# Last block's self-attention: the second maximum of a step issued behind VectorE's copies of the older step

## The chip, the cores and the metric

The kernel runs on one core of a Trainium2 chip. The metric is the device time of one execution in microseconds (us), the median of several runs. A core has five engines that run side by side, each through its own instructions in their order: TensorE (PE in the profile, matmuls and transposes; PEld are its weight loads), VectorE (DVE), ScalarE (ACT), GpSimd (POOL) and SyncE (SP, which here starts most transfers). Matmuls write to PSUM, a small memory from which VectorE and ScalarE read. An instruction that needs another engine's result waits for it, and everything behind it on its own engine waits too.

## What is computed

Four blocks follow each other on an input of 4 x 512 tokens of width 256, with a context of 4 x 64 tokens. The first three are a cross-attention block, a transformer block (self-attention with heads of 64, cross-attention, gated feed-forward), and four layers of a state-space model. The change lies in the last one, whose self-attention has 16 heads of 16:

```python
def _mha(q_in, kv_in, wq, bq, wk, bk, wv, bv, wo, bo):
    b = q_in.shape[0]
    q = (q_in @ wq.T + bq).reshape(b, -1, HEADS, HD).transpose(0, 2, 1, 3)
    k = (kv_in @ wk.T + bk).reshape(b, -1, HEADS, HD).transpose(0, 2, 1, 3)
    v = (kv_in @ wv.T + bv).reshape(b, -1, HEADS, HD).transpose(0, 2, 1, 3)
    scores = jnp.einsum('bhqd,bhkd->bhqk', q, k) * HD ** (-0.5)
    p = jax.nn.softmax(scores, axis=-1)
    o = jnp.einsum('bhqk,bhkd->bhqd', p, v)
    o = o.transpose(0, 2, 1, 3).reshape(b, -1, WIDTH)
    return o @ wo.T + bo
...
h = _layernorm(x, ln1_g, ln1_b)
x = x + _mha(h, h, sa_wq, sa_bq, sa_wk, sa_bk, sa_wv, sa_bv, sa_wo, sa_bo)
h = _layernorm(x, ln2_g, ln2_b)
x = x + _mha(h, context, ca_wq, ca_bq, ca_wk, ca_bk, ca_wv, ca_bv, ca_wo, ca_bo)
```

All of it is float32.

## The kernel before

Self-attention of both transformer-like blocks is written by `self_stage`, called once with `wide` true (heads of 64, in the second block) and once with `wide` false (heads of 16, in the last block, `layer3`). The order of all instructions is written by hand: the body stands under `tc.manual_schedule()`, and each engine gets its instructions in the order in which the Python code issues them.

The work of the last block is 16 chunks `c` of 128 query and key features, which with `wide` false hold 4 heads each (a head is padded to 32 of the 128 rows, `stride`). A chunk takes `spc` = 4 steps, one for each tile of 128 queries, so there are K = 64 steps. One step `k` does four heads of one query tile:

- `scores(k)` issues four matmuls of 32 rows, two into each of two PSUM tiles `ps_s` (name tag `big`, two buffers, so the tile of half `h` in step k+1 uses the buffer of half `h` in step k). Line L952.
- `softmaxed(k)` does, for each half `h`, the negated row maximum on VectorE (`nm`, L963, both heads of the half at once) and then two exps on ScalarE with the row sums as a second output (`pr`, `rs`, L967; the sums come out in an extra accumulator read). The exps are the last readers of the half's `ps_s`.
- `transposes(k, h)` transposes the half's two tiles of probabilities on TensorE into PSUM (`ps_pt`, tag `pt`, two buffers, L981), four transposes a tile, and copies each to `pT`: half 0 by ScalarE (L984), half 1 by VectorE (L986).
- `through_values(n)` multiplies transposed probabilities by values (`ps_o`, L1000). After eight of them a chunk is complete: `finish` copies it out on ScalarE (`AT`, L1018), spreads the row sums by matmul (`ps_rs`, L1025) and VectorE multiplies (L1035).

The steps are overlapped by one: in step `k` the loop issues transposes of step k-1 around the scores of step `k`. In between it works off pieces from queues held by `Pieces`: projections of query, key and value for a later group (L185, evicted by VectorE at L1818, L1820, L1827), output projections (`ps_wo`, evicted at L921), transposes of normalised features (`ps_tr`, tag `pt` too, evicted as `hT` at L646) and pieces of the layer normalisation (L612 to L622). `work()` issues the matmuls of at most one piece, `evict()` issues the VectorE instructions that empty the pieces issued before and moves the normalisation on by one. The pieces share one PSUM buffer (tag `mi`), except `ps_tr`.

So with `wide` false TensorE's order within step `k` is: transposes(k-1, 0), scores(k), one `through_values`, a first piece, transposes(k-1, 1), one `through_values`, a second piece. VectorE's order is: eviction of the second piece of step k-1, both maxima of step k, in every fourth step a reciprocal of the row sums, eviction of the first piece, the two copies of step k-1. ScalarE's is: two copies of step k-1, four exps of step k, in every fourth step the copy of `AT`.

In the loop below, `K` is 64 and `back` is true from the second step on.

Of the kernel before, what the change touches and what calls it, by code (L numbers as in the profile page):

```python
# [8 lines left out]
F32 = mybir.dt.float32  # L9
AF = mybir.ActivationFunctionType  # L10
ALU = mybir.AluOpType
AX = mybir.AxisListType
# [3 lines left out]
P = 128  # L16
B = 4
T = 512
# [39 lines left out]
class Pieces:  # L58
# [11 lines left out]
    def evict(self, norms=1):  # L70
        for ev, ps in self.pend:
            ev(ps)
        self.pend.clear()
        for _ in range(norms):
            if self.norms and next(self.norms[0], 0) == 0:
                self.norms.pop(0)
# [29 lines left out]
    def until(self, ok):  # L106
        for _ in range(200):
            if ok():
                return
            self.evict()  # L110
            if not ok():
                self.work()
        raise RuntimeError("a piece never comes")
# [11 lines left out]
def kernel(ctx: ExitStack, tc: tile.TileContext, t: dict, out: bass.AP):  # L125
    nc = tc.nc
# [478 lines left out]
    def norm(pool, src, b, xns, bias=None, key=None, tag="xn", lag=1):  # L605


        mv = pool.tile([P, TPB, 2], F32, name="ln_mv", tag="ln_mv", bufs=3)
        rstd = pool.tile([P, TPB], F32, name="ln_rstd", tag="ln_rstd", bufs=3)
        for j in range(TPB):  # L610
            st = pool.tile([P, 6], F32, name="ln_st", tag="ln_st", bufs=4)
            nc.vector.bn_stats(out=st, in_=src[:, b * TPB + j, :])  # L612
            nc.vector.bn_aggr(out=mv[:, j, :], in_=st)
            yield
        nc.vector.tensor_scalar(rstd, mv[:, :, 1], EPS, None, ALU.add)  # L615
        nc.gpsimd.tensor_tensor(rstd, rstd, mhalf, ALU.pow)  # L616
        for _ in range(lag):
            yield
        xn = src if tag is None else pool.tile([P, TPB, D], F32, name=tag, tag=tag)
        for j in range(TPB):  # L620
            i = b * TPB + j
            nc.vector.tensor_scalar(  # L622
                xn[:, j, :], src[:, i, :], mv[:, j, 0:1], rstd[:, j : j + 1], ALU.subtract, ALU.mult
            )
            if bias is not None:
                add_bias(src, bias, i)
            if j == TPB - 1:
                xns[b if key is None else key] = xn
            yield
# [223 lines left out]
    def self_stage(X, pool, psum, wide, project, values, Wo, ln, bias, at_end=None, side=None, follows=None, tail=None, fill=None):  # L853
# [72 lines left out]
        def begin(n):  # L926
            b, g = divmod(n, G)
            if g == 0:
                prep.extend(features(pool, psum, xns, hTs, b, c, ln) for c in range(DC))
            prep.extend(projected(n, 0, k) for k in range(2))  # L930
            prep.extend(value(n, j) for j in range(TPB))
            prep.extend(projected(n, m, k) for m in range(1, 4) for k in range(2))

        def combos(k):

            c, r = divmod(k, spc)
            if wide:
                return [(2 * r + i, j) for i in range(2) for j in range(2)]
            return [(r, j) for j in range(4)]

        prs, nms, sums = {}, {}, {}

        def scores(k):
            c = k // spc
            at["chunk"] = c
            until(lambda: c in qs and c in ks)
            for h in range(2):
                ps = psum.tile([P, 2, T], F32, name="ps_s", tag="big", bufs=2)
                for x in range(2):
                    i, j = combos(k)[2 * h + x]  # L950
                    q = slice(j * stride, (j + 1) * stride)
                    nc.tensor.matmul(ps[:, x, :], qs[c][q, i * P : (i + 1) * P], ks[c][q, :], start=True, stop=True)  # L952
                nms[k, h] = ps

        def softmaxed(k):
            c, r = divmod(k, spc)
            if r == 0:
                sums[c] = pool.tile([P, TPB * hpc], F32, name="rs", tag="rs", bufs=6 if wide else 3)
            rs = sums[c][:, 4 * r : 4 * r + 4]
            for h in range(2):  # L960
                ps = nms.pop((k, h))
                nm = pool.tile([P, 2], F32, name="nm", tag="nm", bufs=4)
                nc.vector.tensor_reduce(nm, ps, AX.X, ALU.max, negate=True)  # L963
                for x in range(2):
                    y = 2 * h + x
                    pr = prs[k, y] = pool.tile([P, T], F32, name="pr", tag="pr", bufs=6)
                    nc.scalar.activation(  # L967
                        pr, ps[:, x, :], AF.Exp, bias=nm[:, x : x + 1], accum_out=rs[:, y : y + 1]
                    )

        def transposes(k, h):
            c, r = divmod(k, spc)
            hc = 2 * c + combos(k)[0][0] // 2
            for x in range(2 * h, 2 * h + 2):
                i, j = combos(k)[x]
                if (hc, j) not in pTs:
                    pTs[hc, j] = pool.tile([P, TPB, W2], F32, name="pT", tag="pT", bufs=2 * hpc)
                pr = prs.pop((k, x))
                pp = psum.tile([P, TPB, P], F32, name="ps_pt", tag="pt", bufs=2)
                for t4 in range(TPB):  # L980
                    nc.tensor.transpose(pp[:, t4, :], pr[:, t4 * P : (t4 + 1) * P], ident)  # L981
                to = pTs[hc, j][:, :, (i % 2) * P : (i % 2 + 1) * P]
                if h == 0:
                    nc.scalar.copy(to, pp)  # L984
                else:
                    nc.vector.tensor_copy(to, pp)  # L986
# [56 lines left out]
        with tc.manual_schedule():  # L1043
            for _ in norm(pool, X, 0, xns, bias):
                pass
            begin(0)
            K = NG * SPG
            lead = 4 if wide else 2
            for k in range(K + 4):
                n, r = divmod(k, SPG)  # L1050
                if fill and k == K - SPG:
                    todo.fill.extend(fill(psum))
                if k < K and r == 0:
                    if n < NG - 1:
                        begin(n + 1)
                    else:
                        if follows:
                            norms.append(follows)
                    if n == NG - 1 and at_end:
                        prep.append((lambda: None, lambda ps: at_end(), None))  # L1060
                    if n % G == 0 and n // G < B - 1:
                        norms.append(norm(pool, X, n // G + 1, xns, bias, lag=6 if side else 1))
                evict()
                back = k and k <= K
                if back:
                    transposes(k - 1, 0)
                todo.work_aside()
                if k < K:
                    scores(k)
                    softmaxed(k)  # L1070
                if back and k % spc == 0:
                    rs = sums[k // spc - 1]
                    nc.vector.reciprocal(rs, rs)
                if wide:
                    work()
                    evict(0)
                todo.go_on(1)
                through_values(lead // 2)
                evict(0)
                if k % 2 or not todo.busy:  # L1080
                    todo.go_on(1)
                todo.work_aside()
                work()
                evict()
                if back:
                    transposes(k - 1, 1)
                todo.go_on(1)
                todo.work_aside()
                through_values(lead // 2)
                evict(0)  # L1090
                work()
                if back and (wide or (k - 1) % 2 == 1):
                    c, r1 = divmod(k - 1, spc)
                    hc = 2 * c + combos(k - 1)[0][0] // 2
                    pv.extend((hc, t4) for t4 in range(TPB))
            if tail:

                more = tail(psum)
                todo.evict(0)
                while at["wo"] < NG or more:  # L1100
                    work()
                    if more and (more[0][2] is None or more[0][2]()):
                        mm, ev, _ = more.pop(0)
                        todo.pend.append((ev, mm()))
                    evict(0)
            until(lambda: at["wo"] == NG)
            while todo.side or todo.aside or todo.pend:
                todo.work_aside()
                evict()
                todo.go_on(1)  # L1110
            assert todo.empty() and not pv
# [943 lines left out]
```

## Time and profile before

| what | us |
|---|---|
| median of 3 runs (4137.86 to 4146.58) | 4141.29 |
| the profiled execution | 4144.32 |
| its span, first to last instruction | 4142.5 |
| the changed stage, 64 steps, in the span | 3467 to 3885 |
| of it: TensorE busy | 384.4 |
| VectorE busy | 290.4 |
| ScalarE busy | 253.4 |
| maxima L963 in the stage: 128 of 1.22 | 150.8 |
| exps L967 in the stage: 256 of 0.69, and their accumulator reads, 256 of 0.20 | 172.6 and 51.9 |
| VectorE's copies L986: 127 of 0.68 | 81.4 |

Busy time is the union of an engine's instructions. Matmuls are pipelined and their ends are modelled, so a TensorE that is busy need not be at its peak; starts are more telling. In a timeline, a row is the start in us, the busy time, engine, line, operation, the tile written and those read, and their shapes; behind it, in brackets, stands how long the engine was idle before, and what ended that. Rows of one line that follow each other are merged (x8 is eight instructions). In a list of waits, a row is: the one that waited, what released it, and then the total in us, the number of waits and the longest.

Four score matmuls appear as eight records, since each float32 matmul is recorded as two.

### The profile page before, as it was taken

The numbers are of one execution on the slowest core, as the hardware profiler recorded it, in microseconds if no ns is written. First come the engines' busy times: TensorE is split into PE (matmuls) and PEld (weight loads), VectorE is DVE, ScalarE is ACT, GpSimd is POOL, SyncE is SP. The second block draws the span as 40 slices with busy tenths as digits, with TensorE's granted clock in tenths as the row PEclk, the third lists the DMA queues.
The fourth block names the chain that finished last, engine by engine and source line by source line (L and its number), as shares of the span: only waits on it lengthen the run. The fifth ranks groups of instructions, "written<-read, shape, count | busy, mean of one in ns | idle before, by whom it ended". The sixth has DMA issues, their size and how long they took to land. (4 is left out here: it accounts for less than half of the span.)

```text
span 4142.5 us, 48645 instructions
## 1 busy us (share of the span) xinstructions
PE 3515.9 (85%) x17616; PEld 2204.8 (53%) x17616; DVE 3033.5 (73%) x2903; ACT 2148.3 (52%) x4366; POOL 2388.4 (58%) x1625
## 2 busy tenths in 40 slices
PE   7989998988898897888888788888887667999889
PEld 4654554545566464555555555555554444555446
DVE  5547567476555633999999999998999996676653
ACT  2345454454212424666666666666666553556422
POOL 2349269076100425899999999999998881000131
PEclk8999999999998998988988898888888778999999
DMA  2023022033100203444444444444443441000000
GB/s 75 11 85 103 25 82 92 17 96 94 44 1 0 66 22 104 152 150 154 153 159 148 150 157 159 158 153 149 158 154 138 143 155 36 1 1 1 1 6 16
DMA packets 140287, 369.93 MB, mean 89 GB/s; under 512 B 20624, under 2 KB 38224, under 8 KB 140048
## 3 DMA queue, kind: packets, MB, share of 16 engines
q1 hardware_dynamic: 136688, 363.58, 26.1%
q10 hardware_dynamic: 3360, 3.25, 0.3%
q8 instruction: 139, 2.28, 0.2%
q14 instruction: 100, 0.82, 0.1%
HBM read 363.50 MB, written 3.28 MB: 89 GB/s over the span
## 5 line engine op out<-in xcount | busy, mean ns | idle before, releaser
L1632 POOL TENSOR_TENSOR dBu<-dtx,bB 128x1022 f32<-128x1022 f32 x512 | 1199.0, 2362 | 65.9 <-DVE ps_dA L1659 65.9
L1659 DVE TENSOR_TENSOR_SCAN ps_dA<-ps_dA,dBu 128x1024 f32<-128x1024 f32 x384 | 878.3, 2287 | 131.6 <-POOL dBu L1632 91.8
L1644 ACT ACTIVATE ps_dA<-dt,A 128x512 f32<-128x512 f32 x1024 | 708.3, 692 | 428.5 <-DVE hC L1666 365.6
L1692 PE MATMUL ps_y<-ident,hC 128*128 128x128 f32 x3072 | 460.7, 302 | 104.1 <-DVE hC L1666 104.0
L1692 PEld LDWEIGHTS ps_y<-ident,hC 128*128 128x128 f32 x3072 | 403.9, 158 | 193.3 <-DVE hC L1666 122.4
L1666 DVE TENSOR_TENSOR hC<-ps_dA,bC 128x1024 f32<-128x1024 f32 x384 | 470.1, 1224 | 25.5 <-issue 0.4
L967 ACT ACTIVATE pr<-ps_s,nm 128x512 f32<-128x512 f32 x512 | 345.2, 686 | 260.2 <-DVE nm L963 260.2
L963 DVE TENSOR_REDUCE nm<-ps_s 128x2 f32<-128x1024 f32 x256 | 301.4, 1218 | 158.5 <-PE ps_s L952 144.2
L1670 POOL TENSOR_TENSOR hP<-hP,bC 128x1024 f32<-128x1024 f32 x128 | 302.1, 2360 | 89.2 <-issue 38.9
L981 PE MATMUL ps_pt<-ident,pr 128*128 128x128 f32 x2048 | 284.9, 279 | 66.9 <-DVE pT L986 33.2
L981 PEld LDWEIGHTS ps_pt<-ident,pr 128*128 128x128 f32 x2048 | 232.2, 142 | 165.0 <-issue 61.7
L1659 DVE TENSOR_TENSOR_SCAN hP<-ps_dA,dBu 128x1024 f32<-128x1024 f32 x128 | 291.8, 2280 | 2.9 <-ACT dBu L1649 2.2
L616 POOL TENSOR_TENSOR ln_rstd<-ln_rstd,const 128x4 f32<-128x4 f32 x24 | 24.4, 1018 | 443.8 <-DVE ln_rstd L615 442.2
L178 PE MATMUL ps_cv<-xp,w_dg 128*128 128x512 f32 x512 | 248.9, 619 | 30.9 <-ACT dBu L1649 25.3
L535 DVE TENSOR_TENSOR_SCAN phb<-pdA,phb 128x512 f32<-128x512 f32 x128 | 223.8, 1763 | 60.3 <-POOL phb L525 43.8
L984 ACT COPY pT<-ps_pt 128x512 f32<-128x512 f32 x256 | 140.6, 592 | 171.5 <-PE ps_pt L981 170.9
L1000 PE MATMUL ps_o<-pT,V 128*64 128x256 f32 (+1 forms) x2048 | 221.8, 393 | 1.8 <-ACT AT L1018 1.8
L952 PE MATMUL ps_s<-kT,qT 64*128 64x512 f32 (+1 forms) x1024 | 208.3, 644 | 2.2 <-DVE kT L1172 1.4
L525 POOL TENSOR_TENSOR phb<-hT_res,pm 128x512 f32<-128x512 f32 x128 | 188.4, 1476 | 34.0 <-DMA pm<-scrp 20.9
L1692 PE MATMUL ps_y<-ident,hP 128*128 128x128 f32 x1024 | 154.1, 300 | 54.6 <-POOL hP L1670 54.6
L784 POOL TENSOR_TENSOR pr<-pr,rs 128x512 f32<-128x512 f32 x64 | 65.4, 1043 | 225.2 <-DVE rs L782 219.3
L1692 PEld LDWEIGHTS ps_y<-ident,hP 128*128 128x128 f32 x1024 | 132.2, 155 | 109.6 <-POOL hP L1670 63.1
(276 smaller groups left out, 6399.2 us busy)
## 6 DMA issues: line engine op xcount, KB each, us to landing
bB<-scr SPq DMA_DIRECT2D x256, 512.0 KB, 4.1
bC<-scr SPq DMA_DIRECT2D x256, 512.0 KB, 3.8
pm<-scrp SPq DMA_DIRECT2D x224, 256.0 KB, 3.1
w_pw_in<-in_L_in SPq DMA_DIRECT2D x7, 512.0 KB, 4.5
X<-in_x SPq DMA_DIRECT2D x4, 512.0 KB, 7.2
w_L_W<-in_L_W SPq DMA_DIRECT2D x2, 1024.0 KB, 10.4
w_L_Wq<-in_L_Wq SPq DMA_DIRECT2D x2, 1024.0 KB, 6.4
w_L_Wo<-in_L_Wo SPq DMA_DIRECT2D x2, 1024.0 KB, 9.0
```

Source lines behind the costliest of these rows:

```text
L178: nc.tensor.matmul(dst, l, r, start=(i == 0), stop=(i == len(pairs) - 1))
L535: nc.vector.tensor_tensor_scan(hb, dA, hb, 0.0, ALU.mult, ALU.add)
L963: nc.vector.tensor_reduce(nm, ps, AX.X, ALU.max, negate=True)
L967: nc.scalar.activation(pr, ps[:, x, :], AF.Exp, bias=nm[:, x : x + 1], accum_out=rs[:, y : y + 1])
L981: nc.tensor.transpose(pp[:, t4, :], pr[:, t4 * P : (t4 + 1) * P], ident)
L1000: nc.tensor.matmul(ps_o[0][j * stride : (j + 1) * stride, half * W2 : (half + 1) * W2], Vs[n][0][:, t4, h * stride : (h + 1) * stride], pT ...
L1632: nc.gpsimd.tensor_mul(dBu[:, :, 1:], dtx[:, 1:].unsqueeze(1).broadcast_to([P, 2, T - 1]), bmap[i // 2, 0][:, :, 1:])
L1644: nc.scalar.activation(dA, dt, AF.Exp, scale=A[:, l, m, s : s + 1])
L1659: nc.vector.tensor_tensor_scan(to, dA, dBus.pop(i).rearrange("p s t -> p (s t)"), 0.0, ALU.mult, ALU.add)
L1666: nc.vector.tensor_mul(hCs[i], dA, bmap[i // 2, 1])
L1670: nc.gpsimd.tensor_mul(hCs[i], hCs[i], bmap[i // 2, 1])
L1692: nc.tensor.matmul(y[:, j, k * P : (k + 1) * P], hC[:, s, j * P : (j + 1) * P], ident, is_transpose=True, start=False, stop=(2 * s2 + s == ...
```

## The change

`softmaxed` now takes the half `h` as a parameter and does one half. The first half is issued where both were. With `wide` true the second follows at once, as before. With `wide` false it is issued later in the step, behind `transposes(k - 1, 1)`: on VectorE the second maximum comes behind the reciprocal, the eviction of the step's first piece and the two copies of step k-1. Its two exps are issued there too; since no other ScalarE instruction lies in between, ScalarE's order doesn't change.

```diff
-        def softmaxed(k):
+        def softmaxed(k, h):
             c, r = divmod(k, spc)
-            if r == 0:
+            if r == 0 and h == 0:
                 sums[c] = pool.tile([P, TPB * hpc], F32, name="rs", tag="rs", bufs=6 if wide else 3)
             rs = sums[c][:, 4 * r : 4 * r + 4]
-            for h in range(2):
-                ps = nms.pop((k, h))
-                nm = pool.tile([P, 2], F32, name="nm", tag="nm", bufs=4)
-                nc.vector.tensor_reduce(nm, ps, AX.X, ALU.max, negate=True)
-                for x in range(2):
-                    y = 2 * h + x
-                    pr = prs[k, y] = pool.tile([P, T], F32, name="pr", tag="pr", bufs=6)
-                    nc.scalar.activation(
-                        pr, ps[:, x, :], AF.Exp, bias=nm[:, x : x + 1], accum_out=rs[:, y : y + 1]
-                    )
+            ps = nms.pop((k, h))
+            nm = pool.tile([P, 2], F32, name="nm", tag="nm", bufs=4)
+            nc.vector.tensor_reduce(nm, ps, AX.X, ALU.max, negate=True)
+            for x in range(2):
+                y = 2 * h + x
+                pr = prs[k, y] = pool.tile([P, T], F32, name="pr", tag="pr", bufs=6)
+                nc.scalar.activation(
+                    pr, ps[:, x, :], AF.Exp, bias=nm[:, x : x + 1], accum_out=rs[:, y : y + 1]
+                )
...
                 if k < K:
                     scores(k)
-                    softmaxed(k)
+                    softmaxed(k, 0)
+                    if wide:
+                        softmaxed(k, 1)
...
                 if back:
                     transposes(k - 1, 1)
+                if k < K and not wide:
+                    softmaxed(k, 1)
                 todo.go_on(1)
```

## The prediction

> **What bounds the kernel now.** I read the page first, then the table of stages, the waits inside the last block's self-attention, and last the timeline of single steps. The change touches only that stage: 64 steps from 3467 to 3885 us of a span of 4142.5.
>
> ```profile
> 3467.00:3885.00 418.00, 384.37 (x3316) 219.97 (x3316) 290.39 (x398) 253.37 (x655) 22.79 (x27) 1.00 0.00 1
> PE ps_pt L981 <- DVE pT L986: 21.3, 24, 1.6
> PE ps_pt L981 <- DVE hT L646: 6.4, 6, 1.6
> PE ps_s L952 <- DVE kT L1820: 0.8, 1, 0.8
> ```
>
> First line: TensorE (PE) is busy 384 of 418 us, VectorE (DVE) 290, ScalarE (ACT) 253, granted clock 1.00, no DMA. The others are PE's waits in the stage (total, times, longest). Most are transposes that wait for VectorE's copies; the scores never wait for an exp. The first wait is what the change goes for. The absence of the other is what I doubt will last.
>
> A step with no extra piece of work (a "bare" step), start and duration in us:
>
> ```profile
> 3558.67 1.14 PE L952 MATMUL ps_s<-kT,qT 32*128 32x512 f32 x8
> 3559.74 0.64 PE L1000 MATMUL ps_o<-pT,V 128*32 128x256 f32 x8
> 3559.84 2.36 DVE L963 TENSOR_REDUCE nm<-ps_s 128x2 f32<-128x1024 f32 x2 [1.19 <-PE ps_s L952]
> 3560.31 1.09 PE L981 MATMUL ps_pt<-ident,pr 128*128 128x128 f32 x8
> 3561.16 0.69 ACT L967 ACTIVATE pr<-ps_s,nm 128x512 f32<-128x512 f32 x1 [1.75 <-DVE nm L963]
> 3561.84 0.68 ACT L967 ACTIVATE pr<-ps_s,nm 128x512 f32<-128x512 f32 x1
> 3562.11 1.28 DVE L986 COPY pT<-ps_pt 128x512 f32<-128x512 f32 x2
> 3562.50 0.69 ACT L967 ACTIVATE pr<-ps_s,nm 128x512 f32<-128x512 f32 x1
> 3562.94 1.23 PE L981 MATMUL ps_pt<-ident,pr 128*128 128x128 f32 x8 [0.97 <-DVE pT L986]
> 3563.16 0.69 ACT L967 ACTIVATE pr<-ps_s,nm 128x512 f32<-128x512 f32 x1
> 3563.74 0.21 ACT L967 ACTIVATION_READ_ACCUMULATOR pr<-ps_s,nm 128x1 f32 x1
> 3564.10 1.14 PE L952 MATMUL ps_s<-kT,qT 32*128 32x512 f32 x8
> ```
>
> The step lasts 5.43 us (3558.67 to 3564.10), 0.97 of it PE waiting for the copies that stand behind both maxima. But a second clock runs beside it: `ps_s` has two buffers, and the step's second score tile, filled from 3558.67, is given back when the fourth exp and its accumulator read end at 3563.95, 5.28 us later. The next step wants it at 3564.10. The slack is 0.15 us.
>
> A step whose first piece is a query projection:
>
> ```profile
> 3616.14 1.14 PE L952 MATMUL ps_s<-kT,qT 32*128 32x512 f32 x8
> 3617.37 2.35 DVE L963 TENSOR_REDUCE nm<-ps_s 128x2 f32<-128x1024 f32 x2 [1.94 <-PE ps_s L952]
> 3617.78 1.98 PE L185 MATMUL ps_q<-hT,w_L_q 128*128 128x512 f32 x4
> 3619.60 1.04 PE L981 MATMUL ps_pt<-ident,pr 128*128 128x128 f32 x8
> 3619.80 0.75 DVE L1818 TENSOR_SCALAR qT<-ps_q,cols 128x512 f32<-128x512 f32 x1
> 3620.47 1.28 DVE L986 COPY pT<-ps_pt 128x512 f32<-128x512 f32 x2
> 3620.69 0.69 ACT L967 ACTIVATE pr<-ps_s,nm 128x512 f32<-128x512 f32 x1
> 3623.03 1.14 PE L952 MATMUL ps_s<-kT,qT 32*128 32x512 f32 x8
> ```
>
> Here PE is never idle (6.89 us of work in a step of 6.89), VectorE waits for PE, and the exps are over at 3621.47. Copies come only 4.33 us after the scores, since PE does the projection first.
>
> **The change part by part.** Nothing is added or removed: 128 maxima (1.22 us each) and 256 exps remain, and the built order of PE, ScalarE, GpSimd and SyncE is the same instruction by instruction; no DMA moves. On VectorE alone, 64 second maxima move behind the eviction of the step's first piece and the two copies of step k-1. In the first block's stage both calls still stand together, so it costs nothing there.
>
> *What is taken away.* In the bare step the copies no longer wait for the second maximum. They can start with their transposes, so PE's 0.97 us before the next transposes goes. Over the stage that is at most the 21.3 + 6.4 us shown.
>
> *What it adds.* The second maximum now waits for PE's older transposes, and these stand on PE behind the step's scores, whose second pair waits for the score tile that the exps after the previous second maximum give back. That closes a loop. From the start of one second pair of scores to the next:
> - scores to values: 1.07 (3558.67 to 3559.74). The four score matmuls run side by side (8 records in 1.14 us), so a pair alone takes the same time as all four;
> - values to older transposes: 0.57 (3559.74 to 3560.31), plus the first piece where there is one: 1.82 for a 512-wide query or key (3617.78 to 3619.60), about 0.97 for values;
> - transposes to first copy: 0.69 where the copy waited for nothing else (3884.01 to 3884.70), 0.87 behind a query's eviction (3619.60 to 3620.47);
> - two copies: 1.20, as two of 0.68 take 1.28 together, so each lets the next start after 0.60;
> - maximum to exp 1.32 (3559.84 to 3561.16), exp to exp 0.67;
> - last exp to release: 0.79 with its accumulator read (3563.16 to 3563.95), plus 0.05 for the handover, 0.84 together.
>
> Bare: 1.07 + 0.57 + 0.69 + 1.20 + 1.32 + 0.67 + 0.84 = 6.36 us, against 5.43 now. With a query or key first: 6.36 + 1.82 + 0.18 = 8.36, against 6.89 to 7.78. With values first the copy follows its transposes by 0.64: 7.28. A step takes the longer of PE's work and this loop, and the loop wins in nearly all.
>
> *The sum.* Steps from score group to score group on the timeline:
> - 26 bare steps: 146.7 us now, 26 x 6.36 + 0.6 for normalisation pieces that still stand before the copies: 166.0; +19.3.
> - 17 steps with a query or key first: 124.4 now, 17 x 8.36 = 142.1; +17.7.
> - 8 with a short piece first (values, context key): 50.9 now, 8 x 7.28 = 58.2; +7.3.
> - 6 with output projections: 46.8 now; 6.36 + 1.83 - 0.05 = 8.14 (8.37 for the two with a normalisation behind the eviction), 49.3; +2.5.
> - 3 with feature transposes, where the eviction of `hT` no longer waits behind a maximum: 23.0 now. The eviction starts 0.69 after its transposes, the next transposes 0.86 after it, their copy 0.70 later, the maximum 0.60 later: 1.07 + 0.57 + 2.85 + 1.32 + 0.67 + 0.84 = 7.32, three times 22.0; -1.0.
> - the first three, without values: 19.0 now; 5.8 (no copies yet), 6.94 and 7.79 by the same links; +1.5. The last one: 0.
>
> Together +47.3 us. The first maximum, exps 0 and 1, reciprocals (0.24) and statistics cost nothing: they run in VectorE's and ScalarE's idle time before the copies, which the loop makes longer. Without that cover 16 reciprocals cost 4 us. ScalarE's own copies now stand behind the late exps: two of 0.6 end some 0.9 us after the release, while the older transposes need their buffers 1.64 us after it. The next stage starts when the last output projection lands, so the delay passes through.
>
> *Bounds of what no row shows.* The scores have never waited for an exp. If the tile is free at the exp's own end, the link is 0.75; with the 0.18 us between a VectorE eviction and the next matmul (V ends 3633.93, PE 3634.11) it is 0.97. Over 60 steps that is -5 to +8 us; I take 0.84, the accumulator's row. More idle time on PE might lower its clock. It was 1.00 with PE 84% busy (3558 to 3593) and 0.92 in the next stage at 82% (3910 to 4000); 8% on the loop's PE links (2.3 us) is +13 at worst, and I take 0.
>
> [...] Two copies start 0.60 us apart though each lasts 0.68. [...] The repeated 0.97 us gap is a wait for a buffer of `ps_pt`. [...]
>
> The profiled execution took 4144.3 us (span 4142.5 and 1.8 around it), so 4191.6 on its own account. The median of the three runs is 3.0 lower: 4141.3 + 47.3 = 4188.6, say 4189.
>
> **The rivals.**
> 1. *The copies' wait goes and nothing replaces it.* For it: 21.3 us of waits, and VectorE idle 1.19 us before the maxima. Even so the exps bind: exp 0 starts 2.49 after the scores, three more at 0.67 and 0.84 for release give 5.34 a bare step: 26 steps fall by 146.7 - 138.8 = 8, the feature steps by 3, the first by 1: -12, 4129. It decides if the fourth exp stays within 0.15 us of where it is; the order puts it about 1 us later.
> 2. *A lone pair of scores needs half the time.* Then the loop is 0.53 shorter, bare steps 5.83, a query first 7.83, and the steps with 7.78 us of PE work gain or lose nothing: about +19, 4160. Against it: eight records of 0.64 us mean within 1.14 us, so the pairs share the time.
> 3. *PE's clock falls with its idle time*: +13 on top, 4202.
>
> **How the numbers follow.** Loop as summed 0.78, its own range 4176 to 4200; rival 2 0.09; rival 3 and beyond 0.06; rival 1 0.04; within the noise 0.03. The range 4168 to 4203 leaves out rivals 1 and 2 and the far end of 3. A difference under 0.2% (8 us) can't be told from none. Faster 0.04, same 0.03, slower 0.93.
>
> **What would show it.** Right: PE waiting at `ps_s` for the exps, in some 55 steps, where there was no such wait; the `ps_pt` wait for `pT` nearly gone; second maxima right behind the copies; bare steps near 6.36, those with a query or key first near 8.36, PE's clock 1.00; stage near 465 us. Wrong: scores that don't wait, bare steps under 5.5, or a second pair that is done 0.5 us after its start.

## The result, and the profile after

The changed kernel takes 4199.3 us, median of four runs (4196.08 to 4204.24), against 4139.6 for the kernel before on the same chip (4137.6 to 4146.58): a ratio of 1.0138, 95% interval 1.0126 to 1.0150, so 59.7 us slower. The forecast was 47.3 slower, at 4189, in a range of 4168 to 4203. The direction and the mechanism held; the size was 12 us short.

The profiled execution took 4204.2 us, 59.9 more than the one of before. Measured from the second pair of scores of the first step to that of the last, the stage went from 410.9 to 466.7 us: 55.8 of the 59.9 are there. The rest, 1.3 ahead of the stage and 2.9 behind it, lies in code that the change doesn't touch. Over the nine profiled executions of this study the stage begins between 3458.7 and 3468.7, and what lies behind it takes 264.5 to 269.0 us, with the kernel before at the lower end.

The stage in the table of stretches (start and end, length, busy time and instructions of PE, PEld, DVE, ACT and POOL, granted clock, DMA share, GB/s):

```profile
3467.00:3942.00 475.00, 447.12 (x3311) 244.09 (x3310) 293.50 (x397) 251.95 (x655) 22.75 (x27) 0.97 0.00 1
```

The waits in the same stretch (total, times, longest):

```profile
PEld ps_s L952 <- ACT pr L966: 55.7, 51, 1.7
...
PE ps_s L952 <- ACT pr L966: 18.5, 28, 0.9
...
PE ps_pt L980 <- DVE hT L646: 4.8, 6, 1.1
...
PE ps_pt L980 <- DVE pT L985: 0.6, 2, 0.4
```

(The line numbers differ a little from kernel to kernel: the exps are L967 before, L966 here, L968 without their sums.) The wait of 21.3 us for the copies (`ps_pt` for `pT`) is down to 0.6. In its place scores wait for exps, which before they never did: 51 weight loads and 28 matmuls. And the clock is 0.97, where it was 1.00.

TensorE's busy time rose from 384 to 447 us although it does the same work. That is a matter of counting. A pair of scores that runs alone is busy for as long as four matmuls side by side (1.13 us for four records below, 1.14 for eight before), and now the pairs run apart: the group of `ps_s` has 264.2 us on the page of after and 208.3 on that of before, with the same 1024 matmuls.

One bare step, from the timeline (start, duration, engine, line, operation). Other rows are left out, among them a reciprocal and two pieces of the normalisation on VectorE, which fall into its idle time:

```profile
3886.64 1.13 PE L952 MATMUL ps_s<-kT,qT 32*128 32x512 f32 x4
...
3888.68 1.13 PE L952 MATMUL ps_s<-kT,qT 32*128 32x512 f32 x4 [0.92 <-ACT pr L966]
...
3889.74 0.64 PE L999 MATMUL ps_o<-pT,V 128*32 128x256 f32 x8
...
3890.31 1.09 PE L980 MATMUL ps_pt<-ident,pr 128*128 128x128 f32 x8
...
3891.00 1.29 DVE L985 COPY pT<-ps_pt 128x512 f32<-128x512 f32 x2 [1.30 <-PE ps_pt L980]
...
3892.21 1.21 DVE L962 TENSOR_REDUCE nm<-ps_s 128x2 f32<-128x1024 f32 x1
...
3893.54 0.69 ACT L966 ACTIVATE pr<-ps_s,nm 128x512 f32<-128x512 f32 x1 [2.60 <-DVE nm L962]
...
3894.21 0.68 ACT L966 ACTIVATE pr<-ps_s,nm 128x512 f32<-128x512 f32 x1
...
3895.04 1.13 PE L952 MATMUL ps_s<-kT,qT 32*128 32x512 f32 x4 [0.92 <-ACT pr L966]
```

Reading down the starts gives the loop link by link: 1.06, 0.57, 0.69, 1.21, 1.33, 0.67, 0.83, together 6.36 us. The four scores, one group of eight records before, are now two groups of four with 2.04 us between them. PE's 0.97 us gap at the transposes has become 0.92 us at the scores.

### The profile page after: what moved, and what is told of

It is laid out like the page before. It is cut to its first block, busy times and chain, and to the rows that moved or that the text cites. A ratio compares the mean times of both kernels' runs of the same rounds, so it can differ in the third digit from the quotient of the medians.

```text
span 4202.5 us, 48666 instructions
## 1 busy us (share of the span) xinstructions
PE 3582.0 (85%) x17616; PEld 2231.3 (53%) x17616; DVE 3037.8 (72%) x2903; ACT 2146.4 (51%) x4366; POOL 2386.1 (57%) x1625
## 5 line engine op out<-in xcount | busy, mean ns | idle before, releaser
L966 ACT ACTIVATE pr<-ps_s,nm 128x512 f32<-128x512 f32 x512 | 346.4, 686 | 371.5 <-DVE nm L962 339.0
L952 PE MATMUL ps_s<-kT,qT 64*128 64x512 f32 (+1 forms) x1024 | 264.2, 647 | 21.5 <-ACT pr L966 18.5
L985 DVE COPY pT<-ps_pt 128x512 f32<-128x512 f32 x256 | 165.3, 681 | 47.1 <-PE ps_pt L980 46.5
```

The costliest lines, as they stand in the source:

```text
L966: nc.scalar.activation(pr, ps[:, x, :], AF.Exp, bias=nm[:, x : x + 1], accum_out=rs[:, y : y + 1])
```

## Experiments

Each is an edit of the changed kernel or of the kernel before. "Stage" is always from the first second pair of scores to the last; before 410.9, after 466.7. Ratios are to the kernel before on the same chip.

### Are the exps on the loop? Both kernels without the sums

The row sums are left out, and 1.0 stands in their place:

```diff
-                    pr, ps[:, x, :], AF.Exp, bias=nm[:, x : x + 1], accum_out=rs[:, y : y + 1]
+                    pr, ps[:, x, :], AF.Exp, bias=nm[:, x : x + 1], **(dict(accum_out=rs[:, y : y + 1]) if wide else {})
```

and, not shown, a memset of `rs` to 1.0 on GpSimd. In the changed kernel:

> The changed kernel, with the exps of the last block's self-attention issued without their accumulated sums (the row sums are filled with 1.0 instead, so the row sums are left out). Theory A (the new loop is closed over the second pair's exps: scores, values, transposes, copies, maximum, exp, exp, release): an exp without its sum should start the next about 0.59 us later instead of 0.67 and give its bank back about 0.72 us after its start instead of 0.84, so each of some 61 steps falls by about 0.18 us, a bare step from 6.36 to about 6.2, and the kernel by about 11 us against the changed kernel, to about 4188 us. Theory B (the added time is not on that loop, but is for instance TensorE's clock alone or the transfers): exps are waited for by nobody, the time stays within 2 us of the changed kernel's 4199 us.

In the kernel before:

> The kernel before, with the same exps issued without their sums (row sums filled with 1.0, so the row sums are left out). Theory A (before, the loop is closed by TensorE's own work and by the copies, not by the exps): within 2 us of the kernel before, about 4140 us. Theory B (a faster exp is worth its saving wherever it stands): the same 11 us as in the changed kernel, about 4129 us.

The changed kernel fell to 4182.6 us, ratio 1.0101 (1.0086 to 1.0116) against 1.0138; by the medians that is 17 us less, where 11 were expected. From its timeline:

```profile
3874.45 1.26 ACT L968 ACTIVATE pr<-ps_s,nm 128x512 f32<-128x512 f32 x2 [2.78 <-DVE nm L964]
...
3875.77 1.13 PE L952 MATMUL ps_s<-kT,qT 32*128 32x512 f32 x4 [0.73 <-ACT pr L968]
```

Exps start 0.59 apart instead of 0.67, the second pair of scores starts 0.73 after the start of the last exp instead of 0.82, and every loop-bound kind of step is 0.18 us shorter: bare 6.17, query or key first 8.16, values first 7.09. That is 11.2 us over 62 steps, as theory A has it. The stage fell by 14.2; the other 3 us fit TensorE's clock (six windows at half clock in the stage instead of eight, on which more below), though no run here tests that.

The kernel before took 4144.1, ratio 1.0009 (1.0000 to 1.0018), with the stage at 411.6: nothing gained. The median is 3.9 over the kernel before, where at most 2 were expected. The 0.7 us more in the stage is in steps that now take 5.48 instead of 5.43, and some three more microseconds in the median lie outside the stage and are not explained. So the same saving on the same 256 instructions is worth 11 us in one order and nothing in the other.

### Which part of the move costs? Two positions in between

The second maximum behind the first eviction, ahead of both copies (an edit of the changed kernel):

```diff
                 evict()
+                if k < K and not wide:
+                    softmaxed(k, 1)
                 if back:
                     transposes(k - 1, 1)
-                if k < K and not wide:
-                    softmaxed(k, 1)
```

> The kernel before, with the second maximum and its exps issued after the first half's eviction of the piece of work but ahead of the two copies of the older step: half of the change's move. Theory A (what costs is that the second maximum stands behind the copies, which wait for transposes, which stand behind the values): the loop over the second bank is then about 1.2 + 0.6 + 0.7 us shorter, a bare step stays at TensorE's 5.43 us, and only steps with the query and key projections first lengthen, by about 0.5 us each: the kernel about 3 us over the kernel before, 4140 to 4147 us. Theory B (any second maximum that is issued later starves the scores): tens of us slower, 4165 us or more.

And between the two copies, through a call inside `transposes` (again an edit of the changed kernel):

```diff
-        def transposes(k, h):
+        def transposes(k, h, between=None):
...
             for x in range(2 * h, 2 * h + 2):
+                if between and x % 2:
+                    between()
                 i, j = combos(k)[x]
...
+                second = k < K and not wide
                 if back:
-                    transposes(k - 1, 1)
-                if k < K and not wide:
+                    transposes(k - 1, 1, (lambda: softmaxed(k, 1)) if second else None)
+                elif second:
                     softmaxed(k, 1)
```

> The changed kernel, with the second maximum and its exps issued between the two copies of the older step instead of behind both. Theory A (the two copies stand in the loop at about 0.6 us each): each step that the loop sets is 0.6 us shorter than in the changed kernel, a bare one about 5.74 us between second pairs of scores against 6.36, so the stage loses about 36 us of the 45 that the loop added: the kernel about 12 us over the kernel before, about 4152 us, up to 4158 if some windows at half clock come along. Theory B (it is the last copy's wait, or the order of the banks, and not the copies' time): close to the changed kernel, 4190 to 4200 us.

| second maximum | median us | ratio (95%) | stage us | bare step | query or key first, row sums second |
|---|---|---|---|---|---|
| beside the first (before) | 4140.2 | 1 | 410.9 | 5.43 | 6.89 |
| ahead of the copies | 4147.7 | 1.0015 (1.0006 to 1.0024) | 415.7 | 5.43 | 7.44 |
| between them | 4158.0 | 1.0041 (1.0027 to 1.0055) | 425.0 | 5.76 | 7.74 |
| behind them (the change) | 4199.3 | 1.0138 (1.0126 to 1.0150) | 466.7 | 6.36 | 8.34 |

From the timeline of the kernel with the maximum between the copies:

```profile
3560.83 0.69 DVE L987 COPY pT<-ps_pt 128x512 f32<-128x512 f32 x1
...
3561.43 1.22 DVE L962 TENSOR_REDUCE nm<-ps_s 128x2 f32<-128x1024 f32 x1
...
3562.56 0.68 DVE L987 COPY pT<-ps_pt 128x512 f32<-128x512 f32 x1
...
3563.39 0.63 PE L982 MATMUL ps_pt<-ident,pr 128*128 128x128 f32 x4 [0.92 <-DVE pT L987]
```

The maximum starts 0.60 after the first copy, so one copy is taken out of the loop and a bare step falls by just that, 6.36 to 5.76 (5.74 expected). It also shows the price of the middle: the second copy now stands behind a maximum, and PE waits 0.92 us for it again. The loop is shorter, but at 5.76 still longer than the 5.43 of before.

Ahead of both copies, and apart from one step at half clock, it is the steps with a piece first that lengthen, one with a query or key and the row sums from 6.89 to 7.44. A bare step has no eviction there, so (but for reciprocals and normalisation pieces) its order on VectorE is that of before, and its 5.43 shows nothing about a delay. What can be read is the difference between the rows: standing behind the eviction costs 4.8 us in the stage, standing behind the copies too, with their transposes and the values ahead of them, another 51, of which some 8 are TensorE's clock (below).

The 5.43 of before is itself a loop and not TensorE's work, which is 5.43 less the wait of 0.97. It runs from the scores to the first maximum (1.17), over both maxima to the first copy (2.27), from there to the next transposes (0.83) and to the next scores (1.16), by the starts 3558.67, 3559.84, 3562.11, 3562.94 and 3564.10 in the rows of the prediction. The change took the second maximum out of this loop and closed the longer one.

The median of the first is just past the far end of what was expected (4140 to 4147): its stage is 4.8 over before instead of about 3, 0.6 of it from one window at half clock. The stage of the second is 14.1 over instead of 12, without a window at half clock. Its median is 17.9 over; the difference lies outside the stage and isn't explained.

### The last 9 us: TensorE's clock

The granted clock of after is 0.5 in eight windows of 3.4 us within the stage; before has none there. An extra matmul, never read, ahead of the scores:

```diff
+        BARE = {*range(13, 19), *range(29, 35), *range(45, 48), 49, 50, *range(54, 63)}
...
                 ps = psum.tile([P, 2, T], F32, name="ps_s", tag="big", bufs=2)
+                if h == 0 and not wide and k - 1 in BARE:
+                    nc.tensor.matmul(ps[:, 0, :], qs[c][:, :P], ks[c], start=True, stop=True)
```

> The changed kernel, with one more full-array matmul (queries by keys of the step's own chunk) ahead of the scores of a step that follows a bare one, into the bank that the first pair of scores then overwrites: work for TensorE in its idle time, whose result is never read. Theory A (about 9 us of the added time in the stage, and some 4 us around it, is TensorE's clock, halved for 3.4 us after each sparse window of 3.4 us): the eight windows at half clock in the stage go, to at most two, and the kernel falls by 7 to 13 us against the changed kernel, to about 4190 us. Theory B (the half clock has nothing to do with how sparse TensorE's work is, or the filler is itself in the way): as many windows as before, and the time the same or longer.

It took 4191.5 us, ratio 1.0121 (1.0106 to 1.0137). Two windows at half clock were left of eight, and the stage took 460.9: 5.8 us less. More work for TensorE made the kernel no slower, and the stage faster. The last two windows lay in steps that had no filler, so `BARE` got 1 and 53 as well:

> The kernel with the filler, with the same extra matmul (never read) ahead of the scores of steps 2 and 54 as well, where two windows at half clock were left. Theory A (TensorE's clock halves after a window in which it has too little to do; the new loop costs its own 47 us and the windows the rest): no window at half clock is left in the stage, step 2 falls from 9.47 to about 7.8 us, step 54 from 7.56 to about 6.4, and the stage, from the first second pair of scores to the last, from 460.9 to about 458 us: 47 us over the kernel before, which is the loop alone. Theory B (those two windows have another cause, such as the projections' start): they stay, and the stage stays at about 461 us. By the medians 3 us, which is near what a measurement can tell; the stage decides.

The time is 4189.9 us, ratio 1.0120 (1.0104 to 1.0137). By the medians this last step can't be told from none; the stage can tell it. Its row (from the first scores to the last):

```profile
3458.60:3916.40 457.80, 447.69 (x3320) 241.95 (x3322) 287.59 (x391) 248.74 (x643) 22.74 (x27) 1.00 0.00 1
```

The clock is 1.00, step 2 takes 7.77 and step 54 6.35, and the stage 457.7: 46.8 us over before, the loop without the clock. In the changed kernel itself the clock thus costs 466.7 - 457.7 = 9.0 us in the stage.

What sets it off? Three windows of the changed kernel, each with the one behind it (same columns as above):

```profile
3588.01:3591.42 3.41, 2.64 (x17) 0.73 (x16) 2.63 (x7) 3.04 (x9) 0.00 (x0) 1.00 0.02 5
3591.42:3594.84 3.42, 3.42 (x22) 2.18 (x19) 2.00 (x3) 0.72 (x3) 0.00 (x0) 0.50 0.00 0
3707.47:3710.89 3.42, 2.65 (x17) 0.76 (x16) 2.68 (x7) 2.99 (x9) 0.00 (x0) 1.00 0.00 0
3710.89:3714.30 3.41, 3.41 (x22) 2.08 (x19) 1.91 (x3) 0.76 (x4) 0.00 (x0) 0.50 0.00 0
3898.64:3902.06 3.42, 2.50 (x15) 1.05 (x13) 2.92 (x5) 2.17 (x6) 0.72 (x1) 1.00 0.00 0
3902.06:3905.47 3.41, 3.41 (x20) 1.77 (x16) 0.59 (x2) 1.59 (x5) 0.72 (x1) 0.50 0.02 5
```

One window of the kernel before, with the one behind it:

```profile
3576.50:3579.91 3.41, 1.81 (x22) 1.03 (x17) 3.38 (x7) 2.40 (x7) 0.00 (x0) 1.00 0.02 5
3579.91:3583.33 3.42, 3.40 (x30) 1.90 (x31) 2.06 (x4) 1.55 (x4) 0.00 (x0) 1.00 0.00 0
```

And one of the kernel with more filler:

```profile
3895.21:3898.63 3.42, 3.37 (x19) 0.92 (x18) 1.81 (x3) 2.41 (x7) 0.00 (x0) 1.00 0.03 5
3898.63:3902.04 3.41, 3.41 (x34) 2.12 (x26) 2.47 (x4) 1.44 (x4) 0.00 (x0) 1.00 0.00 0
```

TensorE's busy time doesn't decide it: 1.81 us of 3.41 before, with no drop behind it, and 2.50 to 2.65 after, with one. In the windows shown ahead of a drop TensorE was idle for 0.9 us at most (3.42 - 2.50), all gaps together. In the new loop, lone pairs of scores (two matmuls and no others beside them) fill most of the busy time of the windows ahead of a drop. The share of such a window in which TensorE did anything but scores, worked out from its records, was at most 0.25 for all eight in the changed kernel, the six in the changed kernel without sums and the two left by the first filler. Five other windows of the first two were that sparse, and no drop followed. Where the filler ran in windows just as poor in other work, TensorE was busy some 0.98 of them and none followed. There is one drop of another kind: in the kernel with the maximum ahead of the copies, behind a window with 1.80 us of busy time and no lone pair, but one idle gap of 1.61 us. The window of the kernel before shown above has a gap of 1.61 us too, and 1.81 us of busy time, and no drop followed. So filling the sparse windows stopped the drops (eight, then two, then none), but that a window is sparse doesn't foretell one. What sets a drop off stays open.

### An order that shortens the loop of before

In the loop of before, what stands ahead of the copies on VectorE makes a step longer: normalisation pieces, mostly in bare steps, and in steps 5, 21 and 37 the second maximum ahead of the eviction of `hT`, for which transposes wait. Here the normalisation moves behind the copies (`evict(0)` empties pieces and leaves the normalisation where it is), and in these three steps the second maximum moves behind the eviction of `hT`, still ahead of the copies. An edit of the changed kernel:

```diff
+        LATE = () if wide else (5, 21, 37)
...
                     softmaxed(k, 0)
-                    if wide:
+                    if k not in LATE:
                         softmaxed(k, 1)
...
-                evict()
+                evict(wide)
+                if k in LATE:
+                    softmaxed(k, 1)
                 if back:
                     transposes(k - 1, 1)
-                if k < K and not wide:
-                    softmaxed(k, 1)
+                if not wide:
+                    evict()
```

> The order of before, but the second eviction of a piece of work in the last block's self-attention is issued after the two copies of the older step, and in the three steps 5, 21 and 37 (which evict the transposes of the features) the second maximum stands behind the first eviction, ahead of the copies. Theory A (in the kernel before the transposes wait for the copies only where a normalisation or such an eviction stands ahead of them): steps with a normalisation fall to TensorE's 5.43 to 5.53 us and the three steps by about 0.7 us each: about 6.6 us under the kernel before, 4133 us. Theory B (those steps are held by something else, or what is moved is late for its own readers): 4138 to 4145 us.

From its timeline, a step with a reciprocal and two normalisation pieces:

```profile
3574.08 0.24 DVE L1075 RECIPROCAL rs<-rs 128x16 f32<-128x16 f32 x1
3574.23 1.22 DVE L986 COPY pT<-ps_pt 128x512 f32<-128x512 f32 x2
3575.01 1.22 PE L981 MATMUL ps_pt<-ident,pr 128*128 128x128 f32 x8 [1.08 <-DVE pT L986]
3575.37 0.42 DVE L612 BATCH_NORM_STATS2 ln_st<-X 128x6 f32<-128x256 f32 x1
```

The statistics (L612) stand behind the copies. The step takes 5.53 us, where it took 6.07, and the three `hT` steps 7.14, where they took 7.67. The stage is 404.7 us, 6.2 less, of 6.6 expected. By the medians the kernel takes 4137.0 against 4141.2, 4.2 less where 6.6 were expected, ratio 0.9991 (0.9982 to 0.9999): faster, though hardly more than a measurement can tell.

## Why the prediction was right, and where its size was off

The terms of the sum, against the kernel with more filler (the loop alone) and the changed kernel itself, in us over before:

| steps | forecast | loop alone | changed kernel |
|---|---|---|---|
| 26 bare | +19.3 | +19.5 | +25.1 |
| 17 query or key first | +17.7 | +17.4 | +17.4 |
| 8 short piece first | +7.3 | +7.2 | +8.8 |
| 6 output projections | +2.5 | +2.4 | +2.4 |
| 3 feature transposes | -1.0 | -1.1 | -1.0 |
| first three | +1.5 | +1.4 | +3.1 |
| stage | +47.3 | +46.8 | +55.8 |

- *What is taken away.* As forecast: the wait of `ps_pt` for the copies went. It was worth nothing, since the loop is longer than what it freed.
- *What it adds.* The loop was right in every link. The forecast 6.36 for a bare step is what the profile shows, 8.36 is 8.34, 7.28 is 7.27, 7.32 is 7.32. The release, bounded at 0.75 and 0.97 and taken at 0.84, is 0.82. That the loop closes over the exps is shown by the pair without sums, that the copies stand in it by the middle position.
- *The clock.* This is the step that failed in size: "8% on the loop's PE links (2.3 us) is +13 at worst, and I take 0". It measured 9.0 us in the stage. The third rival was therefore no rival but a further term of the sum, and it works differently from how it was priced: not as a somewhat lower clock on all links, but as eight windows at half clock, 27.3 us together, each of which lengthens one step by 0.6 to 1.7 us. That the price of +13, which widened the range to 4203, came near the 9.0 is luck. The forecast read the clock against TensorE's busy share, which went up here (384 of 418 us before, 447 of 475 after); the windows ahead of the eight drops were 73 to 78% busy, but at most a quarter of each was anything other than scores.
- *The signs.* Scores waited at `ps_s` (51 weight loads, some 55 steps forecast) and bare steps took 6.36. The clock was 0.97 and not 1.00. "Stage near 465 us" counts from 3467 to 3885, 418 us, and 47 more; on that count the stage came to 474.
- *Beside the stage.* 47.3 + 9.0 is 56.3, against 55.8 in the stage; of the 59.9 between the two profiled executions, 4.2 lie outside it. That is within the scatter told of above, and what made them up isn't shown.
- *Rivals 1 and 2.* "Nothing replaces it" fell: the scores wait in its place. "A lone pair needs half the time" fell: the timeline has 1.06 us from the second pair to the values behind it.
- *The gap.* The 0.97 us that PE waited for a buffer of `ps_pt` became 0.92 us of waiting at `ps_s`. No run had more buffers.
- *From copy to copy.* The sum took 0.60 us a copy. In the bare step after, the maximum starts 1.21 us after the first of two copies, and in the kernel with the maximum between them it starts 0.60 after one.

## What to carry to other kernels

When an instruction is moved behind others on its engine, don't stop at the wait that this removes: follow the buffer that its result frees, through every engine, back to the instruction itself. If that ring of links is longer than the step is now, it becomes the step, whatever the engines' busy shares say; here it could be summed to 0.02 us a step from rows of the trace before the change. And add the clock as a term of its own where matmuls that ran side by side will run apart: here it cost 9.0 us of the 55.8 in the stage.

## What the runs showed of the hardware

- In the changed kernel, TensorE's granted clock dropped to 0.5 for one window of 3.4 us, eight times, behind windows in which it was 73 to 78% busy, mostly with lone pairs of 32-row matmuls, while in the kernel before it stayed at 1.00 behind one that was 53% busy with groups of four side by side.
- One extra matmul in each of 26 steps, never read, took six of eight such windows away, and the stage got 5.8 us shorter with more work in it; two more matmuls took the last two, and another 3.2 us.
- An exp without its accumulated sum lets the next start after 0.59 us instead of 0.67, and its PSUM buffer is taken up 0.73 instead of 0.82 us after its start.
